# A graph network on one core: another split of the PSUM banks among its streams, and other stream shares

## The chip, the cores and the metric

The kernel runs on one core of one Trainium2 chip. The time is the device time of one execution in microseconds (us). Before the change the median of three runs is 2337.36 us (2331.5 to 2339.77). The engines are called PE (matmuls; PEld is its weight loads), DVE or VectorE, ACT or ScalarE, POOL or GpSimd, and SP, which only issues transfers. PSUM, into which PE writes, has eight banks here, each of 512 f32 for each of 128 partitions.

## The reference: what is computed

32 graphs of 512 nodes with 64 features each pass through four layers. Each layer ends in `x = layernorm(x + layer(x, adj))`.

```python
# layer 0: mean over neighbours
deg = clip(sum(A, 2), 1);  messages = (A / deg) @ x
# layer 1: Chebyshev polynomials of the Laplacian, order 4
L = I - d[:, None] * A * d[None, :]          # d = rowsum ** -0.5
out = sum_k (T_k(L) @ x) @ W_k + bias        # T_k = 2 L T_{k-1} - T_{k-2}
# layer 2: hyperbolic attention over all pairs i, j
x_local = logmap(x_i, x_j)                   # norms, artanh: logarithms and roots
att = sigmoid([x_self, x_local] @ att_W + att_b) * A
out = proj(expmap(sum_j att * x_local, x))
# layer 3: weighted quantiles over a thinned neighbourhood, then an MLP
adj_d = dilate(A > 0, nodemask)              # drop each skip-th neighbour of rows with over 10
agg = 0.25 q25 + 0.5 q50 + 0.25 q75          # of each feature over the neighbours, sorted
out = (relu((x + agg) @ W1 + b1) @ W2 + b2) * mask
```

## The kernel before

Every graph runs through seven lanes of work, and the lanes of several graphs are worked on at the same time, as a software pipeline:

- *front*: loads `A` in four pieces and `x`, transposes `A` on PE, layers 0 and 1. Its Chebyshev step is a round trip: VectorE writes `front_y`, PE multiplies it with `AT`, ScalarE copies the product (`front_uT`), PE transposes it, VectorE reads it into `front_q`.
- *pairs* and *tail*: layer 2. Norms of all pairs as matmuls, logarithms and exponentials on ScalarE (`pairs_EX`, `pairs_RW`), products on VectorE; the tail is short column work, much of it on POOL, and ends in `x3` and its three 16-bit parts `x3h`.
- *graph*: needs only `AT`. It counts and ranks the neighbours, thins them, sorts the nodes by their number of neighbours and numbers the neighbour slots. Its steps go matmul, PSUM bank, ScalarE, and on to the next matmul: `graph_v`, `graph_V`, `graph_junk`, `graph_VP`, `graph_slot`, and last `graph_dist`, which reads a bank four times.
- *gather*: VectorE builds one-hot matrices (`gather_oh`, from `graph_slot`), PE multiplies `x3h` with them, ScalarE copies the result into the arrays `SB` and `SH`.
- *sort*: a sorting network on VectorE over `SB`, then products with weights that PE makes in a bank (`sort_prod`), which PE sums up into the bank `PA`.
- *head* (once for two graphs): the network over `SH`, the products `PRS`, then for both graphs the store and indirect fetch of the ranked rows, and the MLP.

Nothing of this is issued in the order of the program text. While recording is on, every operation goes through `Order.op` (from line 289 on), with the engine, an estimated duration and what it reads and writes. `Order.issue` (from line 361 on) then plays the program with these estimates and lets each engine take, of its operations that are ready, the one with the smallest key. The key is a due time, `due`: for a lane of graph b it is the period (80) times b plus a share that is interpolated between the lane's five knots in `STAGES` (line 1536), by how deep the operation lies in its lane. So `STAGES` says how far the lanes of different graphs are shifted against each other. `LATE` is added to every handover between two engines in the plan. `STAY` is what a due time must be ahead of before PE changes the shape of its tiles (64 or 128 rows or columns). Where the plan has PE idle, `issue` inserts filling matmuls (line 1579) into `PA`. The order found is then fixed: each engine works through its list in order, and the chip's real durations decide who waits.

PSUM tiles are handed out by `bank` (line 587), one tag for each lane, with the number of banks in `BANKS` (line 585): front 1, pairs 2, graph 1, gather 1, sort 1, head 1; `PA` is the eighth. A lane with one bank can't start the next matmul group before the last reader of the bank has finished. All matmuls carry line 569, transposes 574, ScalarE work 550, VectorE work 514, 518, 521, transfers 578 and fetches 582, so groups are told apart by the names of their tiles, which begin with the lane.

Of the kernel before, what the change touches and what calls it, by code (L numbers as in the profile page):

```python
# [239 lines left out]
class Order:  # L240
# [3 lines left out]

    ENGINES = ("PE", "DVE", "ACT", "POOL", "SP")
    HOP = 0.05
    LATE = 0.08
    STAY = 58.8

    def __init__(self, nc, tc):  # L250
        self.nc, self.tc = nc, tc
# [102 lines left out]
    def after(self, d, i, end, full):  # L354

        a, b = self.ops[d], self.ops[i]
        if a[0] == b[0]:
            return end + (a[2] if full and a[0] != "PE" else 0.0)
        return end + a[2] + self.HOP + self.LATE

    def issue(self, period, stage, filler, fill):
# [24 lines left out]
        while len(order) < n:  # L386
# [11 lines left out]
            if e == "PE":  # L398
                pick = min((h[0][0] + (0.0 if c == shape else self.STAY), c) for c, h in shapes.items() if h)[1]
                i = heapq.heappop(shapes[pick])[1]  # L400
# [69 lines left out]
def tile_adj_resnorm(ctx: ExitStack, tc: tile.TileContext, x, adj, nodemask, w1k, b1k, att_w, att_b,  # L470
# [20 lines left out]
    seq = Order(nc, tc)  # L491
# [90 lines left out]
        seq.op("POOL", 1.15, 2.0, lambda: nc.gpsimd.indirect_dma_start(out, None, rows, bass.IndirectOffsetOnAxis(ap=at, axis=0)),  # L582
               [out], [at], behind=[stored])

    BANKS = {"front": 1, "pairs": 2, "graph": 1, "gather": 1, "sort": 1, "head": 1}

    def bank(dtype=F32, home=None):
        lane, seq.lane = seq.lane, home or seq.lane
        t = seq.tile(pools["ps"], [P, 512 if dtype == F32 else 1024], dtype, "bank", bufs=BANKS.get(seq.lane, 2))
        seq.lane = lane  # L590
        return t
# [295 lines left out]
    def transposed(A):  # L887
        AT = seq.tile(pools["at"], [P, T, N], F32, "AT", 2)
        for j in range(T):
            pt = bank()  # L890
            for t in range(T):
                tr(pt[:, t * P:(t + 1) * P], A[j][:, t, :], identf)
            act(AT[:, j, :], pt, AF.Copy)
        return AT

    def graph(nm, AT, m3, res):
# [3 lines left out]
        ts(nbT, AT, 0.0, None, op0=OP.is_gt)  # L900
        tt(diag(nbT), diag(nbT), identb.unsqueeze(1).to_broadcast([P, T, P]), op=OP.is_gt)
        m = bank()[:, :T]
        for t in range(T):
            for k in range(T):
# [15 lines left out]
        for t in range(T):  # L920
            pt = bank()
            for k in range(T):
                mm(pt[:, k * P:], nbT[:, k, t * P:(t + 1) * P], UC[:, :N - k * P], start=(k == 0), stop=(k == T - 1))
            act(v[:, t, :], pt, AF.Abs, bias=c[:, t:t + 1])
            ts(v[:, t, :], v[:, t, :], skip[:, t:t + 1], -1.0, op0=OP.is_equal, op1=OP.mult)
# [579 lines left out]
    def within_bounds():  # L1505

        gm, BT = pools["gm"], B * T
        seq.lane = "graph"
        p1, p2, p3 = bank(), bank(), bank()
        ge = [seq.tile(gm, [P, T, N], F16, "ge", 1, t).rearrange("p t n -> p (t n)") for t in ("nbT", "v")]  # L1510
        ge = [ge[s % 2][:, s // 2 * BT:(s // 2 + 1) * BT] for s in range(K + 1)]
        seq.lane = "check"
        m = M3.rearrange("p b t -> p (b t)")

        for s in range(K + 1):
            ts(ge[s], m, float(s), None, op0=OP.is_gt)
        for s in range(K + 1):
            mm(p1[:BT, s:s + 1], ge[s], onesP[:, 0:1], start=True, stop=True)
        cs = seq.tile(gm, [BT, K + 1], F16, "cs")
        act(cs, p1[:BT, :K + 1], AF.Copy)  # L1520
        mm(p2[:B, :K + 1], graphs[:BT, :], cs, start=True, stop=True)
        off = seq.tile(gm, [B, 2, K + 1], F16, "off")
        for i, op in enumerate((OP.is_gt, OP.is_lt)):
            tt(off[:, i, :], p2[:B, :K + 1], limits[:, i, :], op=op)
        bad = seq.tile(gm, [B, 1], F32, "bad")
        reduce(bad, off.rearrange("p i s -> p (i s)"), OP.max)
        badh = seq.tile(gm, [B, 1], F16, "badh")
        cp(badh, bad)
        mm(p3[:1, 0:1], badh, onesP[:B, 0:1], start=True, stop=True)
        ts(flag, p3[:1, 0:1], 0.0, None, op0=OP.is_gt)  # L1530
# [2 lines left out]

    STAGES = {"front": (-0.67, -0.59, -0.59, -0.4, -0.35), "pairs": (1.01, 1.02, 1.54, 1.44, 1.34),
              "tail": (2.23, 2.13, 2.56, 2.68, 2.58), "graph": (0.84, 1.06, 1.03, 1.48, 2.2),
              "gather": (2.92, 2.89, 2.92, 3.03, 2.93), "sort": (4.18, 4.47, 4.53, 5.09, 6.03),
              "head": (4.54, 5.59, 5.59, 6, 7.54), "ends": (4.04, 4.143, 4.245, 4.348, 4.45),
              "check": (1.75, 1.83, 1.91, 1.99, 2.07)}  # L1540

    nc.scalar.preload_act_table_set("natural_log_exp_and_others")
    with ExitStack() as fast:
# [59 lines left out]
        within_bounds()  # L1603
        seq.issue(80.0, STAGES, stay_active, 0.3)
        seq.lane = "dense"
# [201 lines left out]
def build(inputs):  # L1807
    import numpy as np
    import concourse.bacc as bacc

    nc = bacc.Bacc("TRN2", target_bir_lowering=False, num_devices=1)
    arrays, args = {}, []
    for name in _INS:
        a = np.ascontiguousarray(inputs[name])
        if a.dtype == np.bool_:
            a = a.view(np.uint8)
        arrays[f"in_{name}_dram"] = a
        args.append(nc.dram_tensor(f"in_{name}_dram", a.shape, mybir.dt.from_np(a.dtype), kind="ExternalInput").ap())
    args.append(nc.dram_tensor("out_0_dram", inputs["x"].shape, F32, kind="ExternalOutput").ap())
    with tile.TileContext(nc) as tc:  # L1820
        tile_adj_resnorm(tc, *args)
    return nc, arrays
# [8 lines left out]
```

## Time and profile before

| | |
|---|---|
| median of three runs | 2337.36 us |
| profiled execution | 2326.41 us, span 2324.6 us |
| mean granted clock of PE | 0.994 |
| PE, DVE, ACT, POOL busy | 94%, 91%, 87%, 47% of the span |
| filling matmuls (line 1579, on `zero`) | 591, 79.8 us of busy time |
| transfers | 57.72 MB, mean 25 GB/s |

Busy shares of ScalarE and VectorE are times in which an instruction of theirs runs. PE's matmuls overlap in the records. A group line gives line, engine, operation, tiles and shapes, the count, the busy time, the mean of one in ns, and the engine's idle time just before them with what ended it. A wait line reads: who waited, for whom, us in total, times, longest. The page's chain of work that ended last holds only the last microsecond here and tells nothing of the rest.

### The profile page before, as it was taken

To read this page: it belongs to the slowest core of one execution; us is meant where nothing else is said; L and a number is where in the kernel's file an instruction comes from. 1 tells how busy PE (TensorE), PEld (TensorE's weight loads), DVE (VectorE), ACT (ScalarE), POOL (GpSimd) and SP (SyncE) were. 2 spreads that over 40 slices of the span, in tenths; PEclk is the share of its full clock that TensorE was granted. 3 is DMA by queue.
4 is the path that set the end of the run, shared out by engine and by line. 5 is a ranking of instruction groups with operands and counts; after the bars stand their busy time and mean duration, and the time that the engine had idled before them with its cause. 6 is when DMAs were issued, how large, how long until landed. Compare 5 with 4: busy or idle time off the path is not lost. (4 is left out here: it accounts for less than half of the span.)

```text
span 2324.6 us, 53396 instructions
## 1 busy us (share of the span) xinstructions
PE 2177.0 (94%) x18555; PEld 1504.3 (65%) x18555; DVE 2115.8 (91%) x6952; ACT 2033.9 (87%) x5818; POOL 1098.7 (47%) x2256
## 2 busy tenths in 40 slices
PE   6999999999999999999999999999999999999987
PEld 4666666666666666666666666666666666666655
DVE  4556999999999999999999999999999999999996
ACT  6798989999998989898989989898998989899753
POOL 1133445545464544545445554544555454454431
PEclk9999999999999999999999999999999999999999
DMA  1010001111000110100011111001111000100000
GB/s 45 21 42 12 18 22 31 27 28 31 27 18 21 34 28 26 33 26 20 22 31 28 27 33 26 19 21 32 29 27 33 26 19 17 29 15 8 13 15 14
DMA packets 131716, 57.72 MB, mean 25 GB/s; under 512 B 56140, under 2 KB 129516, under 8 KB 131436
## 3 DMA queue, kind: packets, MB, share of 16 engines
q1 hardware_dynamic: 126432, 50.09, 8.0%
q0 software_dynamic: 3840, 3.94, 0.8%
q8 instruction: 148, 2.42, 0.4%
q14 instruction: 132, 1.08, 0.2%
q10 hardware_dynamic: 1164, 0.18, 0.0%
HBM read 41.86 MB, written 12.32 MB: 23 GB/s over the span
## 5 line engine op out<-in xcount | busy, mean ns | idle before, releaser
L514 DVE TENSOR_TENSOR SB<-SB 128x92 f32<-128x92 f32 (+12 forms) x1312 | 555.3, 448 | 15.3 <-ACT SB L550 6.2
L569 PE MATMUL gather_bank<-gather_oh,tail_x3h 128*64 128x256 f16 (+5 forms) x5376 | 496.5, 318 | 7.4 <-ACT SB L550 7.1
L569 PEld LDWEIGHTS <-tail_x3h 128*64 128x64 bf16 x5376 | 333.9, 110 | 134.4 <-issue 26.2
L569 PE MATMUL pairs_bank<-pairs_FT 67*128 67x512 f32 (+7 forms) x768 | 305.6, 504 | 8.5 <-DVE pairs_L L521 2.7
L518 DVE TENSOR_SCALAR gather_oh<-graph_slot 128x256 f16<-128x256 f16 (+9 forms) x864 | 252.7, 343 | 27.1 <-PE gather_bank L569 23.5
L514 DVE TENSOR_TENSOR SH<-SH 128x288 f32<-128x288 f32 (+18 forms) x880 | 271.2, 342 | 3.8
L569 PE MATMUL front_bank<-front_AT,front_y 128*64 128x256 f32 x1536 | 190.4, 385 | 12.3 <-DVE front_y L514 11.5
L569 PEld LDWEIGHTS pairs_bank<-pairs_FT 67*128 67x128 f32 (+1 forms) x768 | 127.7, 190 | 83.8 <-issue 18.2
L582 POOL DMA_INDIRECT tail_x<-ranked,graph_spot x120 | 136.5, 1137 | 74.5 <-issue 41.4
L569 PEld LDWEIGHTS <-graph_nbT 128*128 128x128 f16 x1536 | 117.4, 98 | 78.3 <-issue 34.2
L569 PEld LDWEIGHTS front_bank<-front_AT,front_y 128*64 128x64 f32 x1536 | 108.1, 137 | 78.1 <-DVE front_y L514 22.2
L813 POOL TENSOR_TENSOR front_rs<-front_var,mhalf 128x4 f32<-128x4 f32 x64 | 81.1, 1267 | 131.4 <-DVE front_var L518 120.2
L569 PE MATMUL graph_bank<-graph_perm,graph_V 128*128 128x512 f16 x512 | 137.4, 379 | 5.3 <-DVE graph_perm L518 2.7
L569 PE MATMUL pairs_bank<-FLS,pairs_Wt 128*128 128x66 f32 x1024 | 125.6, 273 | 0.3
L514 DVE TENSOR_TENSOR pairs_RW<-pairs_RW,pairs_EX 128x640 f32<-128x640 f32 x128 | 104.7, 818 | 22.9 <-ACT pairs_EX L550 14.6
L569 PEld LDWEIGHTS pairs_bank<-FLS,pairs_Wt 128*128 128x128 f32 x1024 | 121.0, 192 | 2.5 <-DVE pairs_Wt L521 1.7
L569 PEld LDWEIGHTS <-tabs 128*128 128x128 f16 x1296 | 84.0, 98 | 48.3 <-issue 17.4
L550 ACT ACTIVATE graph_junk<-graph_bank,graph_keyh 128x512 f16<-128x512 f32 x128 | 88.0, 688 | 21.8 <-PE graph_bank L574 18.0
L569 PE MATMUL graph_bank<-UC,graph_nbT 128*128 128x512 f16 (+3 forms) x512 | 97.5, 303 | 8.4 <-ACT graph_v L550 4.1
L550 ACT ACTIVATE SB<-gather_bank 128x448 f32<-128x448 f32 (+7 forms) x288 | 89.3, 359 | 18.2 <-PE gather_bank L569 11.9
L569 PE MATMUL PA<-identf,sort_prod 128*96 128x128 f32 (+3 forms) x576 | 103.0, 282 | 1.5 <-DVE sort_prod L514 1.5
L541 POOL TENSOR_SCALAR tail_uc<-tail_un 128x4 f32<-128x4 f32 x32 | 20.7, 646 | 176.6 <-ACT tail_junk L550 170.9
(374 smaller groups left out, 6469.5 us busy)
## 6 DMA issues: line engine op xcount, KB each, us to landing
front_A<-in_adj_dram SPq DMA_DIRECT2D x128, 256.0 KB, 2.9
front_xr<-in_x_dram SPq DMA_DIRECT2D x32, 128.0 KB, 2.2
xs<-tail_x SPq DMA_DIRECT2D x32, 128.0 KB, 2.1
out_dram<-head_zo SPq DMA_DIRECT2D x31, 128.0 KB, 2.0
ranked<-sort_ap SPq DMA_DIRECT2D x30, 128.0 KB, 1.9
tail_x<-ranked,graph_spot POOLq DMA_INDIRECT x120, 2.5
out_dram<-tail_ends SPq DMA_DIRECT2D x1, 128.0 KB, 1.9
wk<-in_L_gnn_weight_dram ACTq DMA_DIRECT2D x1, 64.0 KB, 3.3
```

Of the source, the lines that this page charges most:

```text
L514: vec(lambda: nc.vector.tensor_tensor(out, a, b, op=op), out, [a, b])
L518: vec(lambda: nc.vector.tensor_scalar(out, a, s1, s2, op0=op0, **kw), out, [a], True, (s1, s2))
L541: gp(lambda: nc.gpsimd.tensor_scalar(out, a, s1, s2, op0=op0, **kw), out, [a] + [x for x in (s1, s2) if isinstance(x, bass.AP)])
L550: 0.1, lambda: nc.scalar.activation(out, a, f, scale=scale, **kw), [out, accum_out], [a, after] + sc, table)
L569: return nc.tensor.matmul(out, w, a, start=start, stop=stop)
L582: seq.op("POOL", 1.15, 2.0, lambda: nc.gpsimd.indirect_dma_start(out, None, rows, bass.IndirectOffsetOnAxis(ap=at, axis=0)), [out], [at], ...
L813: seq.op("POOL", 1.6, 0.5, lambda: nc.gpsimd.tensor_tensor(y, v, mhalf, op=OP.pow), [y], [v])
```

## The change

The graph lane gets a second bank. To pay for it, the sort lane has no bank of its own any more: its tiles come from the head's tag, so both take turns in one bank. The knots of all lanes but `ends` and `check` are replaced, and so are `LATE` and `STAY`. Apart from the filling matmuls and the table loads, no operation is added, removed or resized; the recorded program is played again with these numbers, and so the fixed order of every engine is another one.

```diff
-    LATE = 0.08
-    STAY = 58.8
+    LATE = 0.085
+    STAY = 44.5
...
-    BANKS = {"front": 1, "pairs": 2, "graph": 1, "gather": 1, "sort": 1, "head": 1}
+    BANKS = {"front": 1, "pairs": 2, "graph": 2, "gather": 1, "head": 1}

     def bank(dtype=F32, home=None):
-        lane, seq.lane = seq.lane, home or seq.lane
+        lane, seq.lane = seq.lane, home or {"sort": "head"}.get(seq.lane, seq.lane)
...
-    STAGES = {"front": (-0.67, -0.59, -0.59, -0.4, -0.35), "pairs": (1.01, 1.02, 1.54, 1.44, 1.34),
-              "tail": (2.23, 2.13, 2.56, 2.68, 2.58), "graph": (0.84, 1.06, 1.03, 1.48, 2.2),
-              "gather": (2.92, 2.89, 2.92, 3.03, 2.93), "sort": (4.18, 4.47, 4.53, 5.09, 6.03),
-              "head": (4.54, 5.59, 5.59, 6, 7.54), "ends": (4.04, 4.143, 4.245, 4.348, 4.45),
+    STAGES = {"front": (-0.75, -0.64, -0.38, -0.18, -0.28), "pairs": (1.06, 1.28, 1.36, 1.44, 1.48),
+              "tail": (1.73, 2.06, 2.5, 2.58, 2.72), "graph": (0.91, 0.97, 1.03, 1.15, 1.37),
+              "gather": (2.76, 2.67, 2.59, 2.61, 2.8), "sort": (4.18, 4.41, 4.68, 5.14, 5.04),
+              "head": (4.18, 4.32, 4.71, 4.87, 5.23), "ends": (4.04, 4.143, 4.245, 4.348, 4.45),
```

## The prediction

> **What bounds the kernel now.** I read the page's busy shares first, then the stretches, then the waits of TensorE and VectorE, then single groups.
>
> ```profile
> PE 2177.0 (94%) x18555; PEld 1504.3 (65%) x18555; DVE 2115.8 (91%) x6952; ACT 2033.9 (87%) x5818; POOL 1098.7 (47%) x2256
> ```
>
> Three engines are nearly full, so the average says little. I cut the execution in four: the filling of the pipeline, two equal parts of its middle, and its emptying (columns: stretch, length, then busy time of PE, PEld, DVE, ACT, POOL).
>
> ```profile
> 0.00:290.00 290.00, 259.93 (x2006) 178.45 (x2006) 181.66 (x629) 238.09 (x626) 90.40 (x303) 1.00 0.10 28
> 290.00:1218.00 928.00, 882.08 (x7563) 606.77 (x7565) 891.40 (x2913) 846.95 (x2432) 471.19 (x930) 0.99 0.10 26
> 1218.00:2146.00 928.00, 884.60 (x7631) 614.05 (x7628) 887.40 (x2900) 850.03 (x2465) 481.17 (x940) 1.00 0.09 25
> 2146.00:2324.60 178.60, 150.34 (x1360) 105.01 (x1358) 155.32 (x515) 98.88 (x298) 55.95 (x84) 0.97 0.06 14
> ```
>
> In the middle VectorE is busy 891.40 + 887.40 = 1778.8 of 1856 us, or 95.8%. PE reads 95.2%, but its rows overlap: counted from start to start, against the usual distance of two matmuls of these shapes, about 11% of the middle is gaps. So VectorE is the nearest to a bound, and the whole is 2115.8 us of its work plus 208.8 us in which it does nothing: 108.3 while filling, 77.2 in the middle, 23.3 while emptying. The work is the same in both kernels; a change must alter the 208.8. The waits show who makes VectorE idle (middle only), and for PE over the whole span how much of it is the graph's one bank:
>
> ```profile
> DVE pairs_RW L514 <- ACT pairs_EX L550: 13.3, 14, 2.2
> DVE gather_oh L518 <- PE gather_bank L569: 9.2, 14, 2.0
> DVE graph_mi L518 <- PE gather_bank L569: 6.0, 3, 2.0
> DVE SB L514 <- ACT SB L550: 5.6, 9, 1.0
> ...
> DVE graph_v L518 <- ACT graph_v L550: 4.5, 7, 0.9
> ```
>
> ```profile
> PE front_bank L569 <- DVE front_y L514: 11.5, 27, 1.3
> PE graph_bank L569 <- ACT graph_slot L550: 10.7, 20, 1.4
> PE front_bank L574 <- ACT front_R L550: 8.7, 14, 1.7
> ...
> PE graph_bank L569 <- ACT graph_v L550: 7.9, 22, 0.8
> ...
> PE sort_bank L569 <- DVE sort_prod L514: 4.4, 9, 1.5
> ```
>
> No single wait is large. What is left of idle time is many short round trips: VectorE hands something to ScalarE or PE, and comes to the instruction that needs the answer before it is there.
>
> **The change part by part.** The counts here are from the order of instructions in the two built kernels; durations are from the profiled execution (span 2324.6, its own time 2326.4, which is 11 us or 0.5% under the median of the runs, 2337.36).
>
> *What stays.* Every arithmetic instruction, transfer and fetch: 5208 activations, 6952 VectorE instructions, 15174 matmuls without the fillers, 278 transfers on SP, 120 on POOL. All of them are re-ordered. On SP the loads of A are moved past stores of xs, ranked and out, which can hold them back; no PE wait on a load of A shows in the trace after the start, and A lands 2.9 us after issue, so I cost it at nothing; its cover is the three buffers of the A tile, and without it each load would cost those 2.9 us. POOL is 47% busy and its re-ordering is hidden behind that idle time.
>
> *Counts that fall.* Changes of the PE's tile shape fall from 544 to 496. The trace has a matmul after such a change start about 0.1 us later than its like: 48 x 0.1 = 4.8 us less of PE. Table loads fall from 127 to 125, 2 x 1.283 us (the ACT_TABLE_LOAD rows) = 2.6 us less of ScalarE. Neither engine is the bound, so these count only in the rival in which PE is.
>
> *Counts that rise.* Waits on PE rise from 2751 to 3026, fillers from 705 to 724. A matmul that waits starts on average 27 ns later than its like where the bank stays (560 rows) and 83 ns later where it changes (981 rows): 275 x 27 to 83 ns = 7 to 23 us of PE at most, some of it hidden. The fillers (79.8 us / 591 = 0.135 us) are 2.6 us, in gaps that exist anyway.
>
> *The graph's second bank.* All waits of PE for the graph's bank come to 27.0 us (62 waits). With two banks the wait for line 550 on graph_v (7.9) and the like shorten. Bounds: 0 if VectorE, which lacks nothing from it, sets the pace; -27 us if all lands. VectorE itself waits only 4.5 us in the middle for graph_v, so I take the end near 0, and let the next item carry what is left.
>
> The page "Perfetto Trace Analysis" of the Trainium skill (section Matmuls) says that independent groups should rotate through different banks so that evacuation overlaps the next group. By that rule alone the sum would be about 2337 - 27 = 2310 us. The same page (section Identifying the Most-Contended Engine) says to improve the engine with the highest occupancy and that a PE's busy share is a poor measure; by that rule, which agrees with the 95.8% of VectorE here, the second bank is worth nothing.
>
> *Sort and head in one bank.* PE waits 4.4 us for sort_prod now, VectorE 2.7 us for sort_bank. In the new order the two lanes' groups stand far enough apart that shortfalls here fall rather than rise (6.1 to 3.5 us by the count below). Bounds -4 to +9 (both waits doubled would be 7.1, and head's 3.6 us for PRS with it); I take 0.
>
> *The new shares (and LATE, STAY).* This moves everything, and is the main term. I counted, for every VectorE instruction that waits, the round trip: from the last VectorE instruction that the answering engine itself waited for, through that engine's work up to the answer (its rows' durations), plus 0.06 us for each of the two handovers (the trace has 0.03 to 0.08). Where the VectorE work that stands between the two is less than that, the difference is a shortfall; idle time already counted covers later ones. It is a count of direct round trips only. Result for VectorE: 123.2 us before, 139.8 after. By eighths of its instructions: before 78.1, then 4.1 to 8.4 each; after 76.3, then 8.0 to 10.3 each. So the filling is 1.8 us better, the rest 18.4 us worse, together **+16.6 us**. The same count before (45 us after the first eighth) is about half of what the trace shows there, so the upper end of this term doubles the rest: 2 x 18.4 - 1.8 = +35; if the real handovers are kinder at each place, 0.
>
> A place that one can follow: the front's Chebyshev step. VectorE writes front_y, PE multiplies, ScalarE copies, PE transposes, VectorE reads in front_q. When VectorE had to wait for it the trip took 3.5 to 3.8 us. The VectorE work between the two has a median of 5.28 us before and 4.31 after (64 places each), so a cover of about 1.5 us shrinks to 0.5. The shortfall there goes from 11.6 to 25.1 us. Likewise the log chain: pairs_RW after ScalarE's own pairs_RW steps goes from 6.1 to 16.8. Against it, graph_c to graph_v has 5.78 us of work between (2.03 before) and its shortfall falls from 10.8 to 1.1, and pairs_RW after pairs_EX falls from 17.9 to 1.7.
>
> *Filling and emptying.* The most by which PE work that must come first exceeds the VectorE work standing before its reader, at the start: 70.1 us before, 69.5 after: no gain in the filling. At the end 120.6 us of VectorE work stood behind the last pairs_L with 119.1 us of PE work left; now 110.7 with 115.6: PE would end later than VectorE's work, up to 5 us more idle. It is partly in the count above; I take 0 and keep +5 for the range.
>
> **Sum**: 0 (graph bank) + 0 (sort and head) + 16.6 (shares) + 0 = +17 us. Against the profiled execution 2326.4 + 17 = 2343; the median of the runs lies 11 us above it, so 2337.4 + 17 = **2354 us**, +0.7%.
>
> **Rivals.**
>
> *PE becomes the bound (slower, more).* The same count for PE as the waiting engine gives 149.3 us before and 195.2 after (front_y 6.2 to 26.3, graph_dist 2.2 to 20.9: the bank now waits for the last four reads of the graph's stream; pairs_L 18.7 to 29.4). For: before, the count's 149 stands near the waits that the trace shows on PE. Against: PE has gaps to absorb it. It would be +45.9 - 4.8 = +41 us: 2378.
>
> *The second bank pays (faster).* PE's waits for the graph's bank go, ScalarE's answers come earlier, and VectorE's middle idle of 77.2 us falls by what PE loses less: -27 us, 2310. For: the graph's stream is ScalarE's biggest reader of PSUM (418.98 us in the middle), and ScalarE's own shortfalls do fall, 205.8 to 201.6. It decides once the middle's VectorE share exceeds (1778.8 / (1856 - 7)) = 96.2%. Against: the thinner cover counted above.
>
> *Nothing that shows.* The fixed order is in effect elastic: what one place loses the next gains. Within 0.3% (7 us, about what a measurement of this kernel tells from no change).
>
> **How the numbers follow.** Forecast 0.46, PE as bound 0.16, second bank 0.27, nothing 0.11. Faster 0.27, same 0.11, slower 0.62. The forecast's own range is 2345 to 2377 (+8 to +40: 35 and 5 at the emptying). Eight in ten must reach into both other sides: low 2337 - 32 = 2305 (the second bank's -27 with the filling's 1.8 and the table loads), high 2337 + 41 + 17 = 2395 (PE's term with VectorE's on top).
>
> **What would show it.** Right: VectorE's share from 290 to 2146 us falls to about 95% (18 us of 1856), filling idle stays near 108, front_q and pairs_RW lead its waits, front_y and graph_dist those of PE, and PE's waits for graph_v and sort_prod nearly vanish. The prediction is wrong if VectorE's share in the middle rises above 96.2%, or if the filling's idle moves by over 10 us, since I read its bound as unchanged. Its weakest point is that chains over three engines are not in the count.

## The result and the profile after

The changed kernel takes 2488.63 us (median of four runs, 2488.0 to 2489.04); the kernel before, on the same chip, 2337.15 us. The ratio is 1.0658, with an interval of 1.0634 to 1.0681: 6.6% slower. The prediction said 2354 us, in a range from 2305 to 2395. The sign was the likeliest one, the time lies 94 us above the range. The granted clock is 0.994 in both profiles, so the clock is not the cause.

The busy shares of the changed kernel:

```profile
PE 2397.9 (96%) x18559; PEld 1675.6 (67%) x18574; DVE 2121.3 (85%) x6952; ACT 2049.9 (82%) x5816; POOL 1039.6 (42%) x2256
```

VectorE works as long as before (2121.3 against 2115.8 us), PE 221 us longer (2397.9 against 2177.0), with the same matmuls but for a few fillers. The same four stretches (columns: stretch, length, busy time of PE, PEld, DVE, ACT, POOL, clock, DMA share, GB/s):

```profile
0.00:290.00 290.00, 264.09 (x1998) 181.15 (x1999) 175.12 (x612) 236.03 (x625) 81.45 (x297) 1.00 0.10 27
290.00:1218.00 928.00, 909.29 (x7061) 636.20 (x7066) 831.86 (x2727) 801.67 (x2291) 420.79 (x876) 1.00 0.09 25
1218.00:2146.00 928.00, 909.02 (x7115) 639.46 (x7120) 832.68 (x2720) 800.99 (x2288) 428.41 (x865) 1.00 0.09 25
2146.00:2487.30 341.30, 315.49 (x2391) 218.78 (x2392) 281.68 (x896) 211.24 (x614) 108.90 (x219) 0.96 0.05 11
```

In the middle PE is busy (909.29 + 909.02) / 1856 = 98.0%, and VectorE fell from 95.8 to 89.7%. VectorE's idle time is 2487.3 - 2121.3 = 366.0 us instead of 208.8: 114.9 while filling, 191.5 in the middle, 59.6 while emptying. PE has become the bound, and not by waiting. The group of the gather has grown (columns: line, engine, operation, tiles, count, busy time, mean of one in ns, idle time before it):

```profile
L569 PE MATMUL gather_bank<-gather_oh,tail_x3h 128*64 128x448 f16 (+5 forms) x5376 | 743.4, 316 | 3.6 <-ACT SB L550 0.6
```

The same group before:

```profile
L569 PE MATMUL gather_bank<-gather_oh,tail_x3h 128*64 128x256 f16 (+5 forms) x5376 | 496.5, 318 | 7.4 <-ACT SB L550 7.1
```

Count and mean of one are the same, 5376 by 316 to 318 ns; only the time in which at least one of them runs went from 496.5 to 743.4 us. Before, they mostly started two at a time; now mostly one after another. A second group, also of 64 columns, has grown with it, here before and after:

```profile
L569 PE MATMUL front_bank<-front_AT,front_y 128*64 128x256 f32 x1536 | 190.4, 385 | 12.3 <-DVE front_y L514 11.5
L569 PE MATMUL front_bank<-front_AT,front_y 128*64 128x256 f32 x1536 | 235.3, 383 | 1.0 <-DVE front_y L514 0.8
```

`e1` and `f4` leave the places of this group in PE's order alone and only make the gather's matmuls run in pairs, and it shrinks to 184.0 us. So its 45 us come with the gather: its matmuls start between single gather matmuls, as in the last lines of the bank shown below. Both groups run partly at the same time, so PE as a whole grew by 221 us and not by the sum of the two. Who pays is in the waits of VectorE (waiting for whom, total us, times, longest); the first line read 23.5 us before:

```profile
DVE gather_oh L518 <- PE gather_bank L569: 155.4, 159, 4.4
DVE pairs_EX L521 <- PE pairs_bank L569: 26.5, 18, 4.8
DVE front_q L514 <- PE front_bank L574: 24.0, 19, 3.4
```

That is 131.9 of VectorE's 157.2 us of new idle time.

**What the order does to a gather bank.** Each gather matmul uses 64 columns of the array and writes one half of its bank's partitions, the lower or the upper. A bank takes 24 matmuls, 12 for each half; only the first of a graph's six banks takes 48, 24 over 256 columns and 24 over 196. In the built kernel before, the two halves alternate in most banks; in the one after, 12 of the lower half stand in a row, then 12 of the upper (24 and 24 in the first bank, but for two or three). Counted over the built order of PE, a gather matmul follows one of the same half in 990 places of 5376 before, and in 4925 after. One bank in the instructions by time (start, length, group, count), before:

```profile
994.66 2.44 PE L569 MATMUL gather_bank<-gather_oh,tail_x3h 128*64 128x448 f16 x24
```

and after, of which three more matmuls follow behind 772.37:

```profile
769.28 3.43 PE L569 MATMUL gather_bank<-gather_oh,tail_x3h 128*64 128x448 f16 x21
```

The start of each of their matmuls, in ns from the first, from the trace's records:

```
before  0 8  190 196  380 385  568 575  757 764  947 953  1136 1142  1325 1332  ...
after   0  215  403  593  782  971  1160  1350  1539 1545  1728 1758  1916 1947  2106 2136  2325  2515  2704  ...
```

Before, a pair starts within 8 ns and the next pair about 190 ns later. After, single matmuls start about 190 ns apart, each as long as a pair. Eight single starts, four pairs and eight single starts are what the changed kernel's trace has in 51 of its 64 banks over 448 columns and in all 96 over 420, 382 and 340. These are 20 starts where an alternating bank has 12, or 1.67 times as many; the whole group measures 743.4 us against 453.2 with alternating halves (`e1`), 1.64 times. The section "Part 3: Packing small matmuls — row/col tiling" of the Trainium skill's page "TensorE: Matmul & The Clock Gate" says that matmuls in different row or column tiles of the array run at the same time, and counts about 4 ns for each further one; the 5 to 8 ns here are near it. This case adds that it takes a matmul of the other half close by in the order.

**How close by.** Four of one half in a row cost nothing. In the kernel before, the banks over 340 columns begin with four of the lower half and four of the upper, and then alternate; these are 186 of its 990 places, in 31 banks. In the trace all 24 matmuls of each of the 31 start as 12 pairs, and the row of all 32 banks reads 64.9 us against 65.5 where `e2` (below) makes all alternate:

```profile
L569 PE MATMUL gather_bank<-gather_oh,tail_x3h 128*64 128x340 f16 x768 | 64.9, 316 | 3.1 <-ACT SB L550 3.1
L577 PE MATMUL gather_bank<-gather_oh,tail_x3h 128*64 128x340 f16 x768 | 65.5, 323 | 3.1 <-ACT SB L558 3.1
```

The widths in the first bank of a graph show what happens. Before, its order is 12 lower and 12 upper over 256 columns, and then lower and upper by turns over 196. The starts in one such bank (ns from the first, `+` joins a pair):

```
256 alone       0  109  219  327  437  546  655  764
256 with 256    873+880  983+1012  1091+1120  1200+1230
256 alone       1340  1449  1558  1667
256 with 196    1777+1782  1885+1892  1995+2001  2104+2110
196 with 196    2214+2219  ...
```

Four matmuls over 196 columns each start beside one over 256, in 31 of 32 graphs, though all those over 256 stand ahead of them in the built order. So a matmul can start ahead of some that stand before it but write the other half. In most banks it is four that do so, and never more; of twelve in a row eight stay alone.

**Why the order changed.** The gather lane's knots before are 2.92, 2.89, 2.92, 3.03, 2.93: the due time falls with depth only in the first and the last quarter. After, 2.76, 2.67, 2.59, 2.61, 2.8, it falls over the whole first half, where most of the matmuls lie, to judge by the 4925 places. Where it falls, the next matmul of the same accumulation has a smaller key than the first of the other half, and the plan goes down one half before it begins the other. The plan does not see what this costs: line 565 gives a matmul of 64 columns 0.25 ns for each column it reads, 112 ns for 448, whichever half stands beside it. That is about half of what a pair takes, and alone it takes about 190 ns.

### The profile page after: what moved, and what is told of

The parts are those of the page before. It is cut to its first block, busy times and chain, and to the rows that moved or that the text cites. A ratio compares the mean times of both kernels' runs of the same rounds, so it can differ in the third digit from the quotient of the medians.

```text
span 2487.3 us, 53567 instructions
## 1 busy us (share of the span) xinstructions
PE 2397.9 (96%) x18559; PEld 1675.6 (67%) x18574; DVE 2121.3 (85%) x6952; ACT 2049.9 (82%) x5816; POOL 1039.6 (42%) x2256
## 4 chain that ended last, share of the span: by engine, by line
PE 75%; ACT 16%; DVE 7%; issue 1%; DMA 0%; ACTq 0%; POOL 0%; POOLq 0%; DVEq 0%
PE gather_bank L569 29%; PE pairs_bank L569 13%; PE front_bank L569 10%; PE graph_bank L569 10%; PE front_bank L574 3%; PE pairs_bank L574 3%; PE head_bank L569 3%; ACT graph_dist L550 2%; ACT graph_slot L550 2%; DVE pairs_Q L514 2%; ACT pairs_EX L550 1%; PE PA L569 1%; DVE SB L514 1%; ACT front_junk L550 1%; DVE pairs_L L521 1%
## 5 line engine op out<-in xcount | busy, mean ns | idle before, releaser
L569 PE MATMUL gather_bank<-gather_oh,tail_x3h 128*64 128x448 f16 (+5 forms) x5376 | 743.4, 316 | 3.6 <-ACT SB L550 0.6
L569 PEld LDWEIGHTS <-tail_x3h 128*64 128x64 bf16 x5376 | 492.9, 110 | 244.1 <-issue 43.7
L514 DVE TENSOR_TENSOR SB<-SB 128x92 f32<-128x92 f32 (+11 forms) x1312 | 547.2, 448 | 14.7 <-issue 3.9
L518 DVE TENSOR_SCALAR gather_oh<-graph_slot 128x256 f16<-128x256 f16 (+9 forms) x864 | 248.2, 341 | 158.2 <-PE gather_bank L569 155.4
L569 PE MATMUL front_bank<-front_AT,front_y 128*64 128x256 f32 x1536 | 235.3, 383 | 1.0 <-DVE front_y L514 0.8
L569 PEld LDWEIGHTS front_bank<-front_AT,front_y 128*64 128x64 f32 x1536 | 145.2, 136 | 41.8 <-DVE front_y L514 1.9
L582 POOL DMA_INDIRECT tail_x<-ranked,graph_spot x120 | 129.6, 1080 | 48.8 <-issue 48.8
L569 PEld LDWEIGHTS <-tabs 128*128 128x128 f16 x1296 | 74.3, 99 | 89.9 <-issue 71.3
L569 PE MATMUL graph_bank<-UC,graph_nbT 128*128 128x512 f16 (+3 forms) x512 | 108.1, 299 | 9.5 <-ACT graph_dist L550 7.4
L574 PE MATMUL pairs_bank<-identf,pairs_L 128*128 128x128 f32 x512 | 94.8, 283 | 7.3 <-DVE pairs_L L521 3.3
L521 DVE SCALAR_TENSOR_TENSOR pairs_L<-pairs_bank,pairs_Q 128x512 f32<-128x512 f32 x128 | 84.9, 682 | 12.5 <-PE pairs_bank L569 11.6
```

The source lines that it names most:

```text
L514: vec(lambda: nc.vector.tensor_tensor(out, a, b, op=op), out, [a, b])
L518: vec(lambda: nc.vector.tensor_scalar(out, a, s1, s2, op0=op0, **kw), out, [a], True, (s1, s2))
L521: vec(lambda: nc.vector.scalar_tensor_tensor(out, a, s, b, op0=op0, op1=op1), out, [a, b], False, (s,))
L569: return nc.tensor.matmul(out, w, a, start=start, stop=stop)
L574: seq.op("PE", 0.12 if a.dtype == F32 else 0.06, 0.16, lambda: nc.tensor.transpose(out, a, ident), [out], [a, ident], (128, 64 if width(a) ...
```

## Experiments

The theory "halves": the loss is the serial gather matmuls, and what is left when they alternate again is the thinner cover that the prediction counted. Its rivals: the new order's waits cost that much by themselves ("cover"), or the two banks do ("banks"). Kernels of one group ran on one chip beside the kernel before; the four groups were on four chips.

**First group: halves put right, halves spoiled, banks alone.** The kernel before took 2330.38 us here. In `e1` the positions that a bank's gather matmuls have in PE's order stay as they are, and the matmuls are dealt to them in the order of the program, in which the halves alternate. All else is as in the changed kernel; 1 same-half place is left. The edit adds 8 lines, so line numbers behind it are 8 higher.

```diff
-        for t, _, i, tab in sorted(order):
+        order, halves = sorted(order), {}
+        for k, o in enumerate(order):
+            engine, names, where = ops[o[2]][0], ops[o[2]][5], ops[o[2]][6]
+            if engine == "PE" and where[0] == "gather" and len(names) > 1:
+                halves.setdefault([n for n in names if "bank" in n][0], []).append(k)
+        for places in halves.values():
+            for k, i in zip(places, sorted(order[k][2] for k in places)):
+                order[k] = (*order[k][:2], i, order[k][3])
+        for t, _, i, tab in order:
```

> The changed kernel, with its order on every engine kept, except that the gather's matmuls of one bank, which write partitions 0 to 63 or 64 to 127, change places among themselves so that the two halves alternate (5180 of 5376 follow one of the other half, instead of 256). Theory 'halves': in the trace of the changed kernel a 128x448 matmul that follows one of its own half starts 0.19 us after it, and two of different halves start together and need 0.19 us as a pair, so the gather's matmuls fall from 743 us busy to about 430 and the time from 2489 to between 2290 and 2360. Rival 'cover' (my prediction's: thinner work between question and answer): the time stays within 10 us of 2489, as none of these distances change. Rival 'banks' (the graph's second bank and the shared one): also unchanged.

Measured: 2351.92 us, ratio 1.0093 [1.0076, 1.0110]. 137 us of the loss are gone. The group and the first wait lines of VectorE and PE in `e1`, each from its view:

```profile
L577 PE MATMUL gather_bank<-gather_oh,tail_x3h 128*64 128x448 f16 (+5 forms) x5376 | 453.2, 316 | 20.6 <-ACT SH L558 14.4 <-ACT SB L558 2.7 <-DVE gather_oh L526 0.5
```

```profile
DVE front_q L522 <- PE front_bank L582: 32.5, 18, 3.4
DVE pairs_EX L529 <- PE pairs_bank L577: 19.1, 17, 4.8
DVE gather_oh L526 <- PE gather_bank L577: 13.0, 17, 3.2
```

```profile
PE front_bank L577 <- DVE front_y L522: 26.4, 22, 1.8
PE front_bank L582 <- ACT front_uT L558: 21.2, 42, 0.7
```

VectorE's wait for the gather bank falls from 155.4 to 13.0 us. What now leads is the front's round trip, the place that the prediction had named. The stretches of `e1`:

```profile
0.00:290.00 290.00, 260.29 (x2051) 176.64 (x2052) 183.06 (x650) 242.06 (x649) 89.74 (x308) 0.98 0.11 28
290.00:1218.00 928.00, 865.08 (x7534) 575.79 (x7540) 881.68 (x2889) 840.70 (x2421) 469.76 (x917) 1.00 0.10 27
1218.00:2146.00 928.00, 862.50 (x7448) 573.43 (x7451) 875.46 (x2871) 843.54 (x2429) 475.52 (x928) 1.00 0.09 24
2146.00:2354.10 208.10, 175.68 (x1530) 125.04 (x1531) 175.45 (x546) 105.46 (x320) 63.66 (x106) 0.93 0.05 12
```

VectorE is at 94.7% in the middle. Its idle time is 106.9 + 98.9 + 32.6 = 238.5 us, 29.7 more than in the kernel before: -1.4 in the filling, +21.7 in the middle, +9.3 in the emptying. Both are profiled executions on different chips, whose spans differ by 29.5 us; on one chip the medians differ by 21.5. The last stretch is also longer here, so some of its 9.3 us belongs to the middle.

`e2` is the same edit on the kernel before (990 same-half places become 21).

> The kernel before with the same exchange: 990 of its gather matmuls follow one of the same half, mostly those of the first group of each graph; here 21 do. Theory 'halves': gather matmuls from 496 us busy to about 430; the time falls by 0 to 40 us, to 2297 to 2337, since VectorE was busy 95.8% of the middle and takes over as the bound. 'Cover' and 'banks': within 7 us of 2337.

Measured: 2326.87 us, 0.9982 [0.9970, 0.9993]. It is the only version below the kernel before, by 0.2%, less than the 0.3% that the prediction set as the mark. Its gather group is busy 465.0 instead of 496.5 us: 31 us of PE bought 3.5 us of time; VectorE, busy 95.7% of the middle here too, sets the pace. The rivals allowed 7 us from the kernel before, so this run does not tell the theories apart.

`e3` gives the kernel before the changed kernel's gather knots and nothing else (4912 same-half places):

```diff
-              "gather": (2.92, 2.89, 2.92, 3.03, 2.93),
+              "gather": (2.76, 2.67, 2.59, 2.61, 2.8),
```

> The kernel before with one line's part changed: the gather's five knots are those of the changed kernel, which fall over the first half of the lane; banks, other knots, LATE and STAY stay. 4912 gather matmuls then follow one of the same half. Theory 'halves': gather busy about 740 us, time 2440 to 2510. 'Cover' and 'banks': between 2320 and 2365.

Measured: 2535.31 us, 1.0882 [1.0860, 1.0904], and the gather group is busy 748.1 us. One of the change's lines alone makes the whole loss and more. It is 25 us above what was expected at most. The count of uncovered round trips that the prediction used, worked out from the built order and shown by no trace, gives 159.1 us for this order, against 139.8 in the changed kernel. That speaks for a place in the plan that does not fit the other lanes; it was not tried by itself.

`e5` gives the kernel before the changed banks, with the old knots (1003 same-half places):

```diff
-    BANKS = {"front": 1, "pairs": 2, "graph": 1, "gather": 1, "sort": 1, "head": 1}
+    BANKS = {"front": 1, "pairs": 2, "graph": 2, "gather": 1, "head": 1}
...
-        lane, seq.lane = seq.lane, home or seq.lane
+        lane, seq.lane = seq.lane, home or {"sort": "head"}.get(seq.lane, seq.lane)
```

> The kernel before with the banks of the changed kernel alone (graph two, sort and head share one); all knots, LATE and STAY stay. 1003 gather matmuls follow one of the same half, as before (990). Theory 'halves': gather busy stays about 497 us and the time within 30 us of 2337. 'Banks': most of the 151 us, 2440 or more. My prediction's step gave the banks 0, with bounds of -27 and +9.

Measured: 2524.21 us, 1.0831 [1.0812, 1.0849], with a gather group of 494.2 us. The halves are as they were, and it is 8.3% slower all the same: the expectation by "halves" failed here. The fillers of `e5`:

```profile
L1579 PE MATMUL PA<-zero 128*128 128x256 bf16 x1572 | 204.0, 275 | 0.1
```

They were 591 with 79.8 us before. The plan puts a filler where it sees PE idle, so this order has PE idle by plan. VectorE is busy 88.1% of the middle, so it does not set the pace either, and the count of uncovered round trips is 258.8 us, 135.6 more than before. So there are two ways to lose 8% in this program: serial matmuls, and, as these numbers suggest but no run shows by itself, an order that fits its banks badly. The changed kernel has the first; `e1` shows that it has little else.

**Second group: half a dose, and the parts in other combinations.** The kernel before took 2363.99 us on this chip, at a lower granted clock (last section). `e17` is `e1` with the exchange for odd graphs only (2464 same-half places):

```diff
-            if engine == "PE" and where[0] == "gather" and len(names) > 1:
+            if engine == "PE" and where[0] == "gather" and where[1] % 2 and len(names) > 1:
```

> The changed kernel with the exchange of the first experiment for every second graph only: 2464 gather matmuls follow one of the same half (4925 in the changed kernel, 1 with the exchange for all). Theory 'halves', with PE as the bound as long as halves don't alternate: about the middle between 2489 and 2352, 2405 to 2435, gather about 598 us busy. If VectorE took over early, the time would lie nearer to 2352, 2352 to 2400.

Measured: 2499.11 us, 1.0575 [1.0553, 1.0596]; gather group 617.1 us. Half of the serial places, but far more than half of the loss. The first wait of PE in `e17` is one that the changed kernel's profile does not show at this size:

```profile
PE pairs_bank L577 <- ACT pairs_EX L558: 58.8, 15, 4.8
```

This fits neither theory, so the same kernel was run again in the third group.

`e12` has the changed kernel's knots, `LATE` and `STAY`, the old banks, and the exchange of `e1` (10 same-half places).

> The changed kernel with the old banks (graph one, sort its own), its new shares kept and the halves made to alternate. Theory 'shares belong to the banks': the count of direct round trips that VectorE's work doesn't cover rises to 202 us (123 before, 137 in the first experiment); the two runs so far gave 1.5 to 2.2 us of time for each us counted, so 2450 to 2505. Rival 'the second bank is worth nothing where VectorE is the bound' (a step of my prediction): within 15 us of 2352.

Measured: 2468.41 us, 1.0445 [1.0424, 1.0466]; gather group 461.6 us, 917 fillers, counted round trips 202.2 us. `e10` is the changed kernel with its first four gather knots put in rising order, which leaves 5 same-half places:

```diff
-              "gather": (2.76, 2.67, 2.59, 2.61, 2.8),
+              "gather": (2.59, 2.61, 2.67, 2.76, 2.8),
```

> The changed kernel with one edit at the cause: the gather's five knots sorted, 2.59 to 2.8, so that they rise. 5 gather matmuls follow one of the same half. If the falling knots were all that was wrong, 2352 as in the first experiment. The count of uncovered round trips says 165 us (137 there), since the order of everything else moves too: 1.5 to 2.2 us for each of the 42 above before gives 2395 to 2425.

Measured: 2450.12 us, 1.0365 [1.0347, 1.0383]; gather group 476.0 us, 819 fillers, count 165.3 us. `e7` is the kernel before, planned with keys that never fall along the dependences inside a gather (15 same-half places):

```diff
+            if lane in ('gather',):
+                key[i] = max([key[i]] + [key[d] for d in o[4] if self.ops[d][6] == o[6]])
```

> The kernel before, planned again with due times of the gather that may not fall along its dependencies (an operation's key is at least that of what it needs), so that the halves alternate from the plan on: 15 follow one of the same half. 'Halves' alone: about 2327, as in the second experiment. The count of uncovered round trips says 133.7 us (123.2 before): 16 to 23 us more, 2346 to 2354.

Measured: 2380.21 us, 1.0073 [1.0050, 1.0097]; gather group 464.0 us, count 133.7 us. Both `e10` and `e7` show that it is the falling due time that puts a half in a row: without it the places are gone. But a new key moves the whole plan, and what the matmuls gain is lost elsewhere. On this chip the three stand in the order of their counts: 133.7, 165.3, 202.2 us counted; +0.7, +3.6, +4.4% measured. The expected times were worked out for a chip like the first; as ratios to its 2330.38 us, `e7` and `e10` lie inside them, and `e12`, expected at 1.051 or more, lies below. The rival for `e12`, a time within 15 us of 2352, fell.

**Third group: the dose on one chip.** The kernel before took 2334.23 us. `f1` is the changed kernel, `f4` the kernel of `e1`, `f2` that of `e17`, and `f3` its mirror, with `where[1] % 2 == 0`.

> The changed kernel once more, so that the doses stand on one chip: 1.06 to 1.075 times before.

> The half dose again (every second graph's halves alternate, here those of odd number), beside the whole and the none on the same chip. If PE were the only bound all the way, the gain is in proportion: the middle of the two, about 1.037 times before. If the fixed order of the other engines takes over in the graphs that PE finishes early (the half dose's first run has PE waiting 58.8 us for pairs_EX of ScalarE), less than a third of the way, 1.05 or more.

> The other half dose: the even graphs alternate. In proportion: 1.037. If the slow graphs alone set the pace of a period of two graphs: 1.05 or more as with the odd ones, and the two gains add up to less than the whole.

> The first experiment again, on this chip: 1.009 times before, plus or minus 0.005; a chip that grants PE a lower clock may give some thousandths more.

| | halves that alternate | gather group busy | time | ratio |
|---|---|---|---|---|
| `f1` | none | 743.4 us | 2489.58 us | 1.0670 [1.0639, 1.0701] |
| `f3` | even graphs | 601.9 us | 2424.93 us | 1.0393 [1.0346, 1.0440] |
| `f2` | odd graphs | 595.4 us | 2411.78 us | 1.0337 [1.0307, 1.0367] |
| `f4` | all | 452.6 us | 2347.52 us | 1.0059 [1.0027, 1.0091] |

The middle between `f1` and `f4` is 2418.6 us; the two half doses lie 6 above and 7 below it. The loss goes with the dose: the two halves save 64.7 and 77.8 us, the whole 142.1. So they add up, and the expectations of 1.05 or more fell. The saving is about half of the 291 us of gather busy time. PE's whole busy time falls by 239 us from `f1` to `f4` and its idle time grows by 101, since VectorE sets the pace again. `f2` is `e17` to the letter, and the wait of 58.8 us that led PE's waits there is 1.1 us here: the excess of `e17` came with that chip, not with the order.

**Fourth group: the combinations again.** They were meant for a chip like the third, to set their sizes beside `e1`. The chip had a low granted clock again (the kernel before 2362.94 us). `g1` is `e12`, `g2` is `e10`, `g3` is `e7`.

> Old banks with the new shares and alternating halves again, on another chip: the first run of this stood on a chip that granted PE a clock of 0.977 and on which the half dose read 1.058 times before, against 1.034 on the other. 'Shares belong to the banks': 1.03 or more; 'second bank worth nothing': 1.000 to 1.015.

> The changed kernel with the gather's knots sorted, again on another chip (1.0365 on the chip of the low clock). If falling knots were all: 1.006 to 1.010; by the count of uncovered round trips (42 us above before, 1.5 to 2.2 us for each): 1.027 to 1.040.

> The kernel before, planned again with gather keys that don't fall, on another chip (1.0073 on the chip of the low clock): by the count 1.007 to 1.010, by the halves alone 0.998.

Measured: 2470.81 us, 1.0445 [1.0392, 1.0498]; 2436.89 us, 1.0301 [1.0266, 1.0337]; 2377.33 us, 1.0045 [1.0023, 1.0068]. The order of the three is the same. `g1` and `g2` lie where the counts put them; `g3` lies between its two expectations and decides nothing. How large they would be beside `e1` stays open, because the half dose showed that a chip like this one can add 2.4 points (1.0575 against 1.0337).

## Why the prediction was wrong

- **The step that failed** is "The work is the same in both kernels; a change must alter the 208.8", and with it "All of them are re-ordered" at no price but waits. The count went by the rows' durations, and the gather row's mean, 318 ns before, did not change. What changed is how many run at once, which is a matter of neighbours in PE's order. So "PE has gaps to absorb it" failed as well: PE's busy time grew by 221 us, and it had stood still for 148 before. This term stood at 0 and measured +142 us (`f1` against `f4`), or +137 from the first result against `e1`.
- **The trace of before showed it.** Two rows of its groups, which the prediction did not use:

```profile
L569 PE MATMUL gather_bank<-gather_oh,tail_x3h 128*64 128x420 f16 x768 | 79.2, 342 | 4.1 <-ACT SB L550 4.0
L569 PE MATMUL gather_bank<-gather_oh,tail_x3h 128*64 128x256 f16 x768 | 79.0, 275 | 0.0
```

  and the second of them in `e2`:

```profile
L577 PE MATMUL gather_bank<-gather_oh,tail_x3h 128*64 128x256 f16 x768 | 52.3, 275 | 0.0
```

  768 matmuls over 256 columns are busy as long as 768 over 420; by the width, an estimate for them is 79.2 x 256 / 420 = 48.3 us. In the built order of before they are the ones that are taken one half after the other, in most graphs all of them; in `e2`, where they alternate, their row reads 52.3 us. They thus cost 79.0 / 52.3 = 1.51 times what they cost when they alternate. As an estimate, all groups like this would be 1.51 x 465.0 = 702 us (743.4 measured), 206 more than before, and PE's work 2177 + 206 = 2383 us, more than the whole span of 2325: PE as the bound.
- **The cover term came out about right.** The prediction had +16.6 us of uncovered round trips. Without the serial matmuls the change costs +21.5 us (`e1`) or +13.3 us (`f4`), 2352 and 2348 us where 2354 was forecast. Its details hold in `e1` as well: VectorE's share in the middle was to fall to about 95% and is 94.7%; the filling was to stay near 108 us and is 106.9; front_y was to go to 26.3 us of PE's waits and reads 26.4; front_q leads VectorE's waits. Missed: pairs_RW shows 3.0 us for its log chain, not 16.8; graph_dist 0.9 us on PE, not 20.9; and the emptying lost 9.3 us where the sum had 0 and the range 5. That the sum fits so closely is in part luck: the log chain's 10.7 us more did not come, and the emptying's did.
- **Sort and head in one bank, and the second graph bank, at 0:** this holds only with the shares that go with them. PE's wait for graph_v falls as expected, from 7.9 to 1.8 us in `e1`. But the same banks under the old knots cost 194 us (`e5`), and the new knots without the banks cost 4.4% (`e12`, `g1`, on the chips with the lower clock). To price the parts one by one was a wrong cut; only the two together can be costed at nothing.
- **The rival "PE becomes the bound" named the right engine by the wrong way.** It priced PE's own waits at +41 us. In the changed kernel those waits are short (front_y 0.8 us, since PE now comes late everywhere); its work grew. The rival "the second bank pays" fell: no run with the second bank is faster than before.
- **Said beforehand to make it wrong** were a VectorE share above 96.2% or a filling that moves by over 10 us; neither happened (89.7%, +6.6 us). The list lacked a rise of PE's busy time with an unchanged list of instructions.

Left open: why `e3` lies 25 us above its expectation, what exactly costs `e5` its 8%, what the low-clock chips add to the half dose, and the parts that were not tried alone: `LATE` and `STAY`, and the second graph bank apart from the bank that sort and head share.

## What to carry to other kernels

Where matmuls use half the array's columns, price a sequence and not an instruction: compare a group's busy time with its count times the mean of one, and look in the built order for runs on the same half. Here runs of four cost nothing, and of twelve in a row eight ran alone. In a list scheduler, a key that falls with depth makes it finish one chain before it starts its twin; that can undo a concurrency which the program text has, while every row's mean stays the same and the scheduler's own estimates do not move. Knots and banks that were fitted together must be judged together.

## What the runs showed of the hardware

- Two 128x448 matmuls on different column halves start 5 to 8 ns apart when they alternate, and the next pair starts about 190 ns later; on the same half each single one starts about 190 ns after the last.
- In the bank after shown above, eight single starts are followed by four pairs and then singles again: the first four of the upper half start beside the last four of the lower, 6 to 31 ns apart, although other matmuls stand between them in the order. The records of this bank do not name the half; in the kernel before the widths do, with four starts over 196 columns beside four over 256 in 31 of 32 graphs. Why it is four, and never more here, is not shown.
- The four chips differ with one and the same kernel: 2330 and 2334 us at a granted clock of 0.99 for the kernel before, 2363 and 2364 us at 0.98. One kernel lost more: the half dose took 2411.78 us at a clock of 0.994 and 2499.11 us at 0.981, 3.6% for 1.3% of clock. In its slower trace PE waits 15 times, 58.8 us together, at one place that costs 1.1 us in the other. So more than the clock differs, and what it is stays open.
